# Seven products instead of eight for the first token block of a gated layer, with weight differences and the last normalizations moved to VectorE

## The chip, the core and the metric

The kernel runs on one core of a Trainium2 chip, in fp32 throughout. The metric is the device time of one execution in microseconds (us), the median of several runs. Five engines work beside each other, each with its own queue in program order: TensorE (PE; its weight loads are shown apart as PEld), VectorE (DVE), ScalarE (ACT), GpSimd (POOL) and SyncE (SP), which issues most of the DMAs.

## The reference

The computation is one transformer block on x of 2 x 1024 tokens by 256, with a context of 2 x 154 by 192 and 16 heads of 64: self attention, cross attention, and a gated feed-forward layer with 1024 hidden columns.

```python
h = _layernorm(x, ln1_g, ln1_b)
x = _attention(h, h, sa_wq, sa_wk, sa_wv, sa_wo, sa_bo) + x
h = _layernorm(x, ln2_g, ln2_b)
x = _attention(h, cond_emb, ca_wq, ca_wk, ca_wv, ca_wo, ca_bo) + x
h = _layernorm(x, ln3_g, ln3_b)
p = h @ ff_w1 + ff_b1
a, gate = (p[..., :D_FF], p[..., D_FF:])
h = a * jax.nn.gelu(gate, approximate=False) @ ff_w2 + ff_b2
return h + x
```

The change touches the last three lines of the layer: the third normalization for the second batch element, and the product with `ff_w2` for the first quarter of the tokens.

## The kernel before, in words

The order of all instructions is written out by hand (`manual_schedule`): what the Python code calls first stands first in each engine's queue. Self attention runs first, then cross attention, then the gated layer, which is a loop over 64 steps `k`. Pieces of neighbouring stages are put into the steps: the first steps still finish the cross attention and its output projection (`out_piece`, added to x by VectorE at L473), and the third normalization of the second batch element runs at steps 7 to 19.

The tokens are taken in four blocks ("pairs") of 512, each of two halves of 256 (`BT`). The hidden columns are taken in eight chunks of 128, so chunk `n` of the run from 0 to 31 is hidden chunk `n % 8` of block `n // 8`. Chunk `n` takes step 2n (`gate_first`) and step 2n + 1 (`gate_second`), and its last product comes in step 2n + 2 (`gate_last`).

The first projection forms, for both halves and for the value and gate columns, a 2 x 2 scheme of block products with seven products in place of eight (L1062), which needs sums and differences of the weights (`weight_sums`) and of the tokens (`token_sums`, four GpSimd instructions, L1045 to L1048). Their results are joined outside TensorE. ScalarE copies the first product (L1081) and does the two Gelus (L1099, L1105). VectorE does the additions: L1085 and L1087 in `gate_first`, L1101 and L1104 in `gate_second`, L1113 in `gate_last`. The products accumulate in the same PSUM banks, so TensorE's second product into a bank comes after VectorE has read the first. GpSimd multiplies value by gate for the second half (L1106) and for the first half (L1115), into the tiles `ub`.

The second projection multiplies the hidden columns by `ff_w2`. For blocks 1 to 3 it is done in seven products as well (`partial`): the 2 x 2 scheme is over even and odd hidden chunks and over the two halves of the output columns. It needs four differences of quarters of `w2` (`column_sums`, 128x512 each, GpSimd, L1153, at steps 18, 20, 24 and 26) and, for every block and every two hidden chunks, four sums of hidden tiles (`row_sums`, GpSimd, L1165 to L1168). For each of two token tiles a product is four matmuls with 128 columns (L1186), and after the products 1, 6, 3 and 7 VectorE adds parts of the result to x (L1195). Block 0 is done in the plain way: for each of four token tiles eight matmuls of 256 columns (L1225), one addition (L1235) and one store. `sums` is the list of this work, and each step takes slots from its front: two matmuls a step for block 0 (steps 16 to 31), one product a step for the later blocks (from step 32).

The buffer for the differences and row sums (`hold_sums`, tile `wx`) takes the place of a ring buffer of the cross attention, which is read for the last time in step 5.

The third normalization of the second batch element has four parts, a pair of token tiles at a time: statistics on VectorE (`stats`, L239 and L240), variance and deviation on GpSimd (`deviation`, L245 and L249), an offset on VectorE (L255) with scale and shift on GpSimd (`normalize`, L266), and the transposes on TensorE (`turn`, L279), whose results ScalarE scales (L294). A pair passes these parts in steps two apart: statistics of the first pair at step 7, deviation at 9, normalization at 11, transposes at 13. The bias of the layer is added to x by GpSimd (L319), one token tile every third step from 13 on.

Of the kernel before, what the change touches and what calls it, by code (L numbers as in the profile page):

```python
# [8 lines left out]
F32 = mybir.dt.float32  # L9
AF = mybir.ActivationFunctionType  # L10
ALU = mybir.AluOpType
AX = mybir.AxisListType

P = 128
# [4 lines left out]
def tile_transformer_block(ctx: ExitStack, tc: tile.TileContext, a: dict, out: bass.AP):  # L19
    nc = tc.nc  # L20
# [3 lines left out]
    B, S, D = x.shape  # L24
# [7 lines left out]
    NT = S // P  # L32
    GT = 4
# [17 lines left out]
    NF = DF // P  # L51
    SH = GH // 2
    TF = 2
# [18 lines left out]
    def sum_tile(name):  # L72

        return ps_o.tile([P, HB], F32, tag="po", name=name)
# [22 lines left out]
    for n in names:  # L97
        k = n_of[n]
# [121 lines left out]
    def norm_pieces(kind, b, first=False):  # L220
# [7 lines left out]
        st = {}  # L228
# [22 lines left out]

        def normalize(t):
            rstd = st["rstd", t]
            off = small.tile([P, 2], F32, tag="off", name=f"off_{ln}_{b}_{t}")
            nc.vector.scalar_tensor_tensor(  # L255
                off, st["mv", t][:, :, 0], -1.0, rstd, op0=ALU.mult, op1=ALU.mult
            )
            pool, tag = (one, "xn") if narrow(kind, b) and not first else (pp_, "P")

            xn = pool.tile([P, nh, 2, D // nh], F32, tag=tag, name=f"xn_{ln}_{b}_{t}")  # L260
            st["xn", t] = xn
            for i in range(2):
                xs = xt[b, order[t + i] // GT][:, order[t + i] % GT, :]
                xs, own = xs.rearrange("p (c d) -> p c d", c=nh), xn[:, :, i, :]
                if not narrow(kind, b) or first and i == 1:
                    nc.gpsimd.tensor_scalar(  # L266
                        own, xs, rstd[:, i:i + 1], off[:, i:i + 1], op0=ALU.mult, op1=ALU.add)
                else:
                    nc.scalar.activation(
                        own, xs, AF.Identity, bias=off[:, i:i + 1], scale=rstd[:, i:i + 1])  # L270
# [837 lines left out]
    def gate_last(n):  # L1108

        pair, f = divmod(n, NF)  # L1110
        pa, pb, pc, own = psum.pop(n)
        product(n, 4, pb, False)
        nc.vector.scalar_tensor_tensor(  # L1113
            own[:, 0, :], pb[:, :BT], biases(n)[0], own[:, 0, :], op0=ALU.add, op1=ALU.add)
        nc.gpsimd.tensor_tensor(ub[pair][0][:, f, :], own[:, 0, :], own[:, 3, :], ALU.mult)  # L1115
        if f == NF - 1:
            if pair:
                early, late = (1, 4, 2), (5, 6, 3, 7)
                if pair == NPR - 1:
                    sums.extend((pair, i, m) for m in early for i in range(TF))  # L1120
                    sums.extend((pair, i, m) for i in range(TF) for m in late)
                else:
                    sums.extend((pair, i, m) for i in range(TF) for m in early + late)
            else:
                sums.extend((pair, i, e) for i in range(2 * TF) for e in range(NF))

    sums, summed = [], {}

# [21 lines left out]
    def column_sums(n):  # L1150

        t = half["t"]
        nc.gpsimd.tensor_tensor(*[  # L1153
            lambda: (t[5], quarter(0, 1), quarter(0, 0)),
            lambda: (t[6], quarter(1, 1), t[5]),
            lambda: (t[4], quarter(1, 0), t[6]),
            lambda: (t[7], quarter(1, 1), quarter(0, 1)),
        ][n](), ALU.subtract)

    def row_sums(pair, c):  # L1160

        s = {i: own[:, c, :] for i, own in half["s"][pair % 2].items()}
        (a11, a12), (a21, a22) = ([ub[pair][j][:, 2 * c + e, :] for e in range(2)] for j in range(2))
        tt = nc.gpsimd.tensor_tensor
        tt(s[5], a21, a22, ALU.add)  # L1165
        tt(s[6], s[5], a11, ALU.subtract)
        tt(s[3], a12, s[6], ALU.subtract)
        tt(a21, a11, a21, ALU.subtract)  # L1168
# [46 lines left out]

    def sum_slot():

        pair, i, f = sums.pop(0)
        if pair:
            return partial(pair, i, f)  # L1220
        if f == 0:
            summed[pair] = sum_tile(f"pf{pair}_{i}")
        own = summed[pair]
        j, e = divmod(i, TF)
        nc.tensor.matmul(  # L1225
            own[:, :D], lhsT=ub[pair][j][:, f, e * P:(e + 1) * P], rhs=w2[:, f, :],
            start=(f == 0), stop=(f == NF - 1),
        )
        if f < NF - 1:
            return None  # L1230
        b, t = divmod(pair * 2 * TF + i, NT)

        def store():
            xs = xt[b, t // GT][:, t % GT, :]
            nc.vector.tensor_tensor(xs, own[:, :D], xs, ALU.add)  # L1235
            nc.sync.dma_start(out=out[b, t * P:(t + 1) * P, :], in_=xs)

        return store


    with tc.manual_schedule():
# [192 lines left out]
        for k in range(2 * FU):  # L1434
# [16 lines left out]
                out_pieces("ca", B - 1, NQ - 1, out_order("ca"))  # L1451
            if k % (2 * NF) == NF and k < 2 * FU - 2 * NF:
                token_sums(k // (2 * NF) + 1)
            for _ in range(min(2 if k < 4 * NF else 1, len(sums))):
                run(sum_slot)
            flush(stores)
            run_work(0 if k in (1, 2 * len(CG) - 1) else 1 + k % 2, k % 2)
            if later and k > 12 and k % 3 == 1:
                later.pop(0)()
            if k == 2 * NF:  # L1460
                hold_sums()
            if k in (2 * NF + 2, 2 * NF + 4, 2 * NF + 8, 2 * NF + 10):
                column_sums((k - 2 * NF) // 3)
            pair, at = divmod(k - 5, 2 * NF)
            if pair > 0 and at % 4 == 0:
                row_sums(pair, at // 4)
# [38 lines left out]
```

## Time and profile before

| | us |
|---|---|
| median of the runs (3) | 1084.04 |
| lowest and highest run | 1083.71, 1085.92 |
| the profiled execution | 1085.11 |
| its span in the profile | 1083.3 |
| TensorE busy in the span | 1067.4 (99%) |
| VectorE, ScalarE, GpSimd busy | 889.9, 646.9, 765.0 |

The profile is one execution. Times in its timelines and windows are microseconds from the start of the span. A line such as L1062 is a line of the kernel before; a name such as `own<-pb` tells which tile is written from which. In a timeline a row gives the start, the duration, the engine, the line, the operation, the tiles, the shapes and the count, and in brackets the idle time before it with what ended it. A 256-wide fp32 product of the program appears as two matmul records.

### The profile page before, as it was taken

The numbers are of one execution on the slowest core, as the hardware profiler recorded it, in microseconds if no ns is written. First come the engines' busy times: TensorE is split into PE (matmuls) and PEld (weight loads), VectorE is DVE, ScalarE is ACT, GpSimd is POOL, SyncE is SP. The second block draws the span as 40 slices with busy tenths as digits, with TensorE's granted clock in tenths as the row PEclk, the third lists the DMA queues.
The fourth block names the chain that finished last, engine by engine and source line by source line (L and its number), as shares of the span: only waits on it lengthen the run. The fifth ranks groups of instructions, "written<-read, shape, count | busy, mean of one in ns | idle before, by whom it ended". The sixth has DMA issues, their size and how long they took to land.

```text
span 1083.3 us, 45246 instructions
## 1 busy us (share of the span) xinstructions
PE 1067.4 (99%) x18548; PEld 710.0 (66%) x18548; DVE 889.9 (82%) x1317; ACT 646.9 (60%) x2063; POOL 765.0 (71%) x1600
## 2 busy tenths in 40 slices
PE   8999999999999999999999999998999999999998
PEld 6556556566565565565675665575777767888998
DVE  5789999998998989999999989968877887655554
ACT  5666767677666666666776766666566554342221
POOL 2667777788777777777777777757665686388774
PEclk9999999999999999999999999999999999999999
DMA  3232111111111111211211201136855545000000
GB/s 94 64 90 62 44 43 44 37 38 43 33 43 24 43 43 33 48 42 29 48 41 26 53 14 37 24 96 139 202 134 138 126 115 131 17 6 15 20 11 30
DMA packets 105120, 62.84 MB, mean 58 GB/s; under 512 B 32266, under 2 KB 95506, under 8 KB 104914
## 3 DMA queue, kind: packets, MB, share of 16 engines
q1 hardware_dynamic: 103586, 59.29, 23.2%
q8 instruction: 146, 2.39, 0.9%
q10 hardware_dynamic: 1328, 0.66, 0.2%
q14 instruction: 60, 0.49, 0.1%
HBM read 30.01 MB, written 2.10 MB: 30 GB/s over the span
## 4 chain that ended last, share of the span: by engine, by line
PE 87%; DVE 3%; DMA 3%; POOL 3%; ACT 2%; SPq 1%; issue 1%; DVEq 0%; POOLq 0%; ACTq 0%
PE s L492 19%; PE po L546 19%; PE py_sa L466 5%; PE py_ca L466 5%; PE pv_sa L392 5%; PE pq_ca L361 4%; PE pq_sa L361 4%; PE pk_sa L361 4%; PE poc L938 4%; PE pb L1062 3%; PE pf L1186 3%; PE sc L855 3%; PE pa L1062 2%; PE pc L1062 2%; DMA st<-st 2%; PE pf L1225 1%
## 5 line engine op out<-in xcount | busy, mean ns | idle before, releaser
L612 POOL TENSOR_SCALAR p<-p,rd,ee 128x512 f32<-128x512 f32 x508 | 387.3, 773 | 99.1 <-DVE rd L604 97.3
L507 ACT ACTIVATE p<-s,st 128x512 f32<-128x512 f32 x512 | 345.8, 686 | 176.5 <-DVE st L501 170.5
L501 DVE TENSOR_REDUCE st<-s 128x2 f32<-128x1024 f32 x256 | 308.5, 1206 | 51.7 <-issue 20.1
L639 DVE STREAM_TRANSPOSE pT<-p 128x1024 f32<-128x1024 f32 x256 | 302.3, 1219 | 1.5 <-POOL p L612 1.5
L492 PE MATMUL s<-k_sa,q_sa 64*32 64x512 f32 x4096 | 255.4, 591 | 2.7 <-ACT p L507 2.1
L546 PE MATMUL po<-pT,v_sa 64*32 64x256 f32 x8192 | 238.6, 376 | 0.9 <-ACT p L873 0.9
L546 PEld LDWEIGHTS po<-pT,v_sa 64*32 64x32 f32 x8192 | 173.8, 106 | 74.9 <-issue 27.3
L492 PEld LDWEIGHTS s<-k_sa,q_sa 64*32 64x32 f32 x4096 | 81.6, 106 | 102.8 <-issue 53.5
L873 ACT ACTIVATE p<-sc,neg 128x154 f32<-128x154 f32 x256 | 96.5, 408 | 84.5 <-DVE rden L881 80.7
L884 POOL TENSOR_SCALAR p<-p,rden 128x154 f32<-128x154 f32 x256 | 97.3, 401 | 62.7 <-DVE rden L881 62.3
L507 ACT ACTIVATION_READ_ACCUMULATOR p<-s,st 128x1 f32 x512 | 103.2, 202 | 0.0
L525 POOL TENSOR_TENSOR dd<-st 128x8 f32<-128x8 f32 x128 | 25.8, 202 | 66.1 <-DMA st<-st 64.3
L392 PEld LDWEIGHTS pv_sa<-sa_wv,hT_ln 64*128 64x128 f32 x1024 | 58.6, 188 | 14.2 <-issue 10.9
L392 PE MATMUL pv_sa<-sa_wv,hT_ln 64*128 64x128 f32 x1024 | 61.8, 275 | 0.0
L860 DVE TENSOR_REDUCE neg<-sc 128x6 f32<-128x924 f32 (+1 forms) x48 | 48.0, 1001 | 14.5 <-PE sc L855 14.4
L466 PE MATMUL py_ca<-ca_wo,o_ca 128*128 128x256 f32 x256 | 59.9, 382 | 0.0
L466 PE MATMUL py_sa<-sa_wo,o_sa 128*128 128x256 f32 x256 | 59.5, 386 | 0.0
L466 PEld LDWEIGHTS py_sa<-sa_wo,o_sa 128*128 128x128 f32 x256 | 47.3, 190 | 17.8 <-issue 6.9
L361 PE MATMUL pq_ca<-hT_ln,ca_wq 64*128 64x512 f32 (+1 forms) x352 | 58.4, 590 | 0.5 <-DMA ca_wq<-in_L_xattn_ca_wq_dram 0.5
L873 ACT ACTIVATION_READ_ACCUMULATOR p<-sc,neg 128x1 f32 x256 | 57.2, 224 | 0.0
L361 PE MATMUL pq_sa<-hT_ln,sa_wq 64*32 64x512 f32 (+1 forms) x976 | 57.0, 586 | 0.0
L361 PE MATMUL pk_sa<-hT_ln,sa_wk 64*32 64x512 f32 x960 | 56.8, 590 | 0.0
(135 smaller groups left out, 1471.5 us busy)
## 6 DMA issues: line engine op xcount, KB each, us to landing
wf<-pT_ca SPq DMA_DIRECT2D x128, 128.0 KB, 2.4
v_sa<-v_sa SPq DMA_DIRECT2D x32, 256.0 KB, 3.8
st<-st SPq DMA_DIRECT2D x510, 1.0 KB, 1.9
sa_wq<-in_L_xattn_sa_wq_dram SPq DMA_DIRECT2D x32, 128.0 KB, 3.4
sa_wk<-in_L_xattn_sa_wk_dram SPq DMA_DIRECT2D x32, 128.0 KB, 3.6
sa_wv<-in_L_xattn_sa_wv_dram SPq DMA_DIRECT2D x32, 128.0 KB, 3.3
ca_wq<-in_L_xattn_ca_wq_dram SPq DMA_DIRECT2D x32, 128.0 KB, 4.4
wf<-in_L_xattn_ff_w_dram SPq DMA_DIRECT2D x12, 256.0 KB, 4.2
```

The costliest lines, as they stand in the source:

```text
L361: nc.tensor.matmul(pq[r][f:f + m, at:at + n], lhsT=wt[own, c, f:f + m], rhs=h[own, c, t0:t0 + n], start=(c == 0), stop=(c == NH - 1), tile ...
L392: nc.tensor.matmul(pv[r][:, i * P:(i + 1) * P], lhsT=h[own, c, i * P:(i + 1) * P], rhs=wt[own, c, :], start=(c == 0), stop=(c == NH - 1), ...
L466: nc.tensor.matmul(py[:, e * D:(e + 1) * D], lhsT=o[:, i, (t + e) * P:(t + e + 1) * P], rhs=wo[kind, b, g][:, i, :], start=(i == 0), stop= ...
L492: nc.tensor.matmul(sc[a4 * KB:(a4 + 1) * KB, j, :], lhsT=q[r, c:c + KB], rhs=k[r, h * HB:(h + 1) * HB], start=True, stop=True, tile_positi ...
L501: nc.vector.tensor_reduce(st[:, 0, 0, i, :], sc, AX.X, ALU.max, negate=True)
L507: nc.scalar.activation(pr[:, j, :], sc[:, j, :], AF.Exp, bias=st[:, 0, 0, i, j:j + 1], accum_out=st[:, 0, 1, i, j:j + 1],)
L546: nc.tensor.matmul(po[a2][d:d + KB, :QH // 2], lhsT=v[r, t, e, d:d + KB], rhs=pT[r, d // DH * NK + n, :], start=(t == 0 and e == 0), stop= ...
L612: nc.gpsimd.tensor_scalar(pr[:, j, :], pr[:, j, :], v["rd"][:, c:c + 1], v["ee"][:, 0, c:c + 1], op0=ALU.mult, op1=ALU.mult,)
L639: nc.vector.transpose(halves[h][:, :, c:c + KB], slot[p]["members"][i].rearrange("p j (n k) -> p (j n) k", k=KB))
L873: nc.scalar.activation(pr_[:, j, i, :T], sc[:, j, i * T:(i + 1) * T], AF.Exp, bias=neg[:, j, i:i + 1], accum_out=den[:, j, i:i + 1],)
L884: nc.gpsimd.tensor_scalar(pr_[:, j, i, :T], pr_[:, j, i, :T], rden[:, j, i:i + 1], 1.0, op0=ALU.mult, op1=ALU.mult,)
L1062: nc.tensor.matmul(into[:, :BT], lhsT=lhs, rhs=wh[pair][i], start=first, stop=True, skip_group_check=True)
```

## The change

The first block's second projection is done in seven products like the others. Its 32 matmuls of 256 columns become 56 of 128 columns, in 14 slots of one product each (steps 16 to 29), the four additions on VectorE become twelve, and the plain path is removed. The row sums of block 0 are added on GpSimd, at steps 8, 10, 14 and 17, four instructions each.

The buffer `wx` is taken at step 7 instead of 16. The four differences of `w2` are done by VectorE instead of GpSimd, at the ends of steps 7, 9, 11 and 13 instead of 18, 20, 24 and 26.

The normalization of the second batch element ahead of the gated layer subtracts the mean and multiplies by the deviation on VectorE, two instructions for a pair of token tiles, in place of one offset on VectorE and two instructions on GpSimd. It stands where the offset stood, at steps 11, 13, 15 and 17.

```diff
         def normalize(t):
             rstd = st["rstd", t]
+            if kind == "ff" and b == B - 1:
+                xn = st["xn", t] = pp_.tile(
+                    [P, nh, 2, D // nh], F32, tag="P", name=f"xn_{ln}_{b}_{t}")
+                for i in range(2):
+                    xs = xt[b, order[t + i] // GT][:, order[t + i] % GT, :]
+                    nc.vector.tensor_scalar(
+                        xn[:, :, i, :], xs.rearrange("p (c d) -> p c d", c=nh),
+                        st["mv", t][:, i, 0:1], rstd[:, i:i + 1],
+                        op0=ALU.subtract, op1=ALU.mult)
+                return
...
         if f == NF - 1:
-            if pair:
-                early, late = (1, 4, 2), (5, 6, 3, 7)
-                if pair == NPR - 1:
-                    sums.extend((pair, i, m) for m in early for i in range(TF))
-                    sums.extend((pair, i, m) for i in range(TF) for m in late)
-                else:
-                    sums.extend((pair, i, m) for i in range(TF) for m in early + late)
+            early, late = (1, 4, 2), (5, 6, 3, 7)
+            if pair == NPR - 1:
+                sums.extend((pair, i, m) for m in early for i in range(TF))
+                sums.extend((pair, i, m) for i in range(TF) for m in late)
             else:
-                sums.extend((pair, i, e) for i in range(2 * TF) for e in range(NF))
+                sums.extend((pair, i, m) for i in range(TF) for m in early + late)
...
     def column_sums(n):
 
         t = half["t"]
-        nc.gpsimd.tensor_tensor(*[
+        nc.vector.tensor_tensor(*[
...
     def sum_slot():
 
-        pair, i, f = sums.pop(0)
-        if pair:
-            return partial(pair, i, f)
...
+        return partial(*sums.pop(0))
...
-            for _ in range(min(2 if k < 4 * NF else 1, len(sums))):
+            for _ in range(min(1, len(sums))):
                 run(sum_slot)
...
-            if k == 2 * NF:
+            if k == NF - 1:
                 hold_sums()
-            if k in (2 * NF + 2, 2 * NF + 4, 2 * NF + 8, 2 * NF + 10):
-                column_sums((k - 2 * NF) // 3)
+            if k in (NF - 1, NF + 1, NF + 3, NF + 5):
+                column_sums((k + 1 - NF) // 2)
+            if k in (NF - 1 + 1, NF + 2, NF + 6, 2 * NF + 1):
+                row_sums(0, (k + 1 - NF) // 3)
```

More of the change, by code (lines that the diff above doesn't have):

```diff
@@ L1216, in sum_slot @@
     def sum_slot():
-        pair, i, f = sums.pop(0)
-        if pair:
-            return partial(pair, i, f)
[L1221 to L1238, printed above, removed]
+        return partial(*sums.pop(0))
     with tc.manual_schedule():
```

## The prediction

> **What bounds the kernel now.** I read the page first, then a table of windows over the gated layer, then the chain of waits through it, and last the timelines of TensorE (PE), VectorE (DVE) and GpSimd (POOL) between 930 and 1000 us.
>
> ```profile
> span 1083.3 us, 45246 instructions
> ...
> PE 1067.4 (99%) x18548; PEld 710.0 (66%) x18548; DVE 889.9 (82%) x1317; ACT 646.9 (60%) x2063; POOL 765.0 (71%) x1600
> ```
>
> TensorE is busy 99% of the span, so a time saved anywhere else shows only where TensorE waits. The windows (stretch, length, then busy time of PE, PEld, DVE, ACT, POOL) say where that is:
>
> ```profile
> 942.10:953.80 11.70, 10.92 (x51) 8.23 (x50) 10.13 (x32) 4.80 (x12) 9.34 (x17) 1.00 0.01 1
> 955.50:994.50 39.00, 39.00 (x186) 34.33 (x186) 19.52 (x46) 13.01 (x29) 34.64 (x49) 1.00 0.04 13
> 994.50:1027.00 32.50, 32.50 (x207) 30.10 (x206) 18.65 (x44) 9.13 (x20) 23.35 (x34) 1.00 0.04 15
> ```
>
> From 955.5 on TensorE has no idle time: the first block's sixteen slots of the second projection and the next block's fourteen are bound by its matmuls. Between 942.1 and 953.8, hidden chunks 4 to 7, whose steps have no second projection to fill them, it is idle 0.78 of 11.70 us, while VectorE is busy 10.13 and GpSimd 9.34. The timeline of VectorE shows why:
>
> ```profile
> 941.88 0.48 DVE L1101 SCALAR_TENSOR_TENSOR own<-pb,cols,own 128x256 f32<-128x256 f32 x1 [0.17 <-PE pb L1062]
> ...
> 945.30 0.48 DVE L1101 SCALAR_TENSOR_TENSOR own<-pb,cols,own 128x256 f32<-128x256 f32 x1 [0.46 <-PE pb L1062]
> ...
> 947.15 0.37 DVE L255 SCALAR_TENSOR_TENSOR off_ln<-mv_ln,rstd_ln 128x2 f32<-128x2 f32 x1
> 947.44 0.47 DVE L1113 SCALAR_TENSOR_TENSOR own<-pb,cols,own 128x256 f32<-128x256 f32 x1
> 947.84 0.41 DVE L1085 TENSOR_TENSOR own<-pb,own 128x256 f32<-128x256 f32 x1
> ...
> 949.04 0.48 DVE L1101 SCALAR_TENSOR_TENSOR own<-pb,cols,own 128x256 f32<-128x256 f32 x1 [0.46 <-PE pb L1062]
> ...
> 950.89 0.37 DVE L255 SCALAR_TENSOR_TENSOR off_ln<-mv_ln,rstd_ln 128x2 f32<-128x2 f32 x1
> ...
> 952.88 0.48 DVE L1101 SCALAR_TENSOR_TENSOR own<-pb,cols,own 128x256 f32<-128x256 f32 x1 [0.44 <-PE pb L1062]
> ...
> 953.65 0.43 DVE L255 SCALAR_TENSOR_TENSOR off_ln<-mv_ln,rstd_ln 128x2 f32<-128x2 f32 x1
> 954.87 0.48 DVE L1113 SCALAR_TENSOR_TENSOR own<-pb,cols,own 128x256 f32<-128x256 f32 x1 [0.80 <-PE pb L1062]
> ...
> 958.23 0.73 DVE L255 SCALAR_TENSOR_TENSOR off_ln<-mv_ln,rstd_ln 128x2 f32<-128x2 f32 x1
> 960.06 0.48 DVE L1113 SCALAR_TENSOR_TENSOR own<-pb,cols,own 128x256 f32<-128x256 f32 x1 [1.09 <-PE pb L1062]
> ```
>
> L1101 of chunk 5 starts at 945.30 and of chunk 6 at 949.04, and all that VectorE does between stands back to back: L1101, L1104, the norm's statistics, the offset L255, L1113, L1085, L1087. TensorE waits for the L1085 in it:
>
> ```profile
> 948.30 0.70 PE L1062 MATMUL pb<-hT_ln,wf 128*128 128x256 f32 x2 [0.45 <-DVE own L1085]
> ...
> 949.70 0.55 PE L279 MATMUL ph_ln<-ident,xn_ln 128*128 128x128 f32 x3 [0.16 <-POOL xn_ln L266]
> ...
> 957.69 1.03 PE L1225 MATMUL pf<-wf,u 128*128 128x256 f32 x4
> ...
> 960.72 1.03 PE L1225 MATMUL pf<-wf,u 128*128 128x256 f32 x4
> ```
>
> L1085 ends at 948.26, the product into the same bank starts at 948.30, and its end lets L1101 start at 949.04. That is a loop: VectorE's work from L1101 to L1085, plus 0.78 us of TensorE's answer. It takes 945.30 - 941.88 = 3.42 us for chunk 4, 3.74 for chunk 5 and 3.84 for chunk 6, where seven products of 0.43 us are 3.0. Each VectorE instruction put into it lengthens the kernel by its whole time. From chunk 7 on there is slack: L1113 at 954.87 waited 0.80 us and at 960.06 1.09 us for TensorE.
>
> **The change, part by part.** First the second projection of the first block. The chain has the price of a slot in both forms (start, length, group):
>
> ```profile
> 948.55 1.11 POOL xn_ln L266 x2
> ...
> 955.70 0.86 PE pf L1225 x4
> ...
> 991.97 0.86 PE pf L1225 x4
> ...
> 994.56 0.89 PE pf L1186 x8
> ```
>
> A slot of the plain form is two 256-wide matmuls, 0.86 us, and there are 16 of them, 13.76 us. A slot of the seven-product form is four 128-wide ones, 0.89 us, and there are 14, 12.46 us. On a TensorE without idle time that is -1.30 us. The narrower stores on VectorE (twelve additions in place of four) lie in steps that have the same slots in the next block, where the window from 994.5 shows TensorE busy throughout, so I cost them at nothing; without that cover each would be in VectorE's slack of some 1.3 us a step.
>
> Second, the four weight differences (128x512 each) go from GpSimd to VectorE, to the ends of steps 7, 9, 11 and 13, behind the gate of chunks 3, 4, 5 and 6. The one at step 7 stands before two residual additions that wait for TensorE's output projection anyway: nothing. The other three stand in the loop. No row has this operation on VectorE; the nearest are these groups (count, busy us and mean ns):
>
> ```profile
> L1195 DVE TENSOR_TENSOR x<-pf,x 128x512 f32<-128x512 f32 x12 | 8.3, 692 | 6.2 <-PE pf L1186 6.2
> ...
> L290 DVE TENSOR_SCALAR hT_ln<-ph_ln,cols 128x256 f32<-128x256 f32 x6 | 3.0, 531 | 0.0
> ...
> L810 DVE MEMSET v_ca<- 128x512 f32 x2 | 1.0, 485 | 0.1
> ```
>
> The same operation with one operand in PSUM takes 0.69 us, a mere 128x512 fill 0.485. I take 0.60, with 0.485 and 0.69 as ends. Beside it there is a wait. The offset L255 reads two tensors in SBUF, as the differences do. In the cross attention, under short GpSimd instructions, it took 0.18 us:
>
> ```profile
> 878.99 0.18 DVE L255 SCALAR_TENSOR_TENSOR off_ln<-mv_ln,rstd_ln 128x2 f32<-128x2 f32 x1
> ```
>
> In the gated layer it took 0.37, 0.37 (at 950.89, as at 947.15), 0.43 and 0.73 us, and GpSimd's rows tell when it came free:
>
> ```profile
> 938.99 0.73 POOL L1115 TENSOR_TENSOR u<-own 128x256 f32<-128x256 f32 x1 [3.11 <-DVE own L1113]
> ...
> 946.78 0.73 POOL L1106 TENSOR_TENSOR kT<-own 128x256 f32<-128x256 f32 x1 [0.94 <-ACT own L1105]
> 947.58 0.19 POOL L245 TENSOR_SCALAR var_ln<-mv_ln 128x2 f32<-128x2 f32 x1
> 947.85 0.69 POOL L249 TENSOR_TENSOR rstd_ln<-var_ln,power 128x2 f32<-128x2 f32 x1
> ...
> 953.33 0.73 POOL L319 TENSOR_TENSOR x<-x,ff_b 128x256 f32<-128x256 f32 x1
> ...
> 958.23 0.73 POOL L319 TENSOR_TENSOR x<-x,ff_b 128x256 f32<-128x256 f32 x1
> ...
> 970.00 0.72 POOL L1165 TENSOR_TENSOR wx<-u 128x256 f32<-128x256 f32 x1
> ...
> 972.98 0.73 POOL L1115 TENSOR_TENSOR u<-own 128x256 f32<-128x256 f32 x1
> ```
>
> The one at 947.15 ends at 947.52, GpSimd's L1106 at 946.78 + 0.73 = 947.51. The one at 953.65 ends at 954.08, L319 at 954.06. The one at 958.23 ends at 958.96 together with L319. So VectorE is held until the running GpSimd instruction ends. The mean of the four is 0.475, so the wait is 0.30 us, and I give that to each difference: 0.90 us. (The Trainium skill, page "SBUF — State Buffer", section "Who interferes with whom", says the same: a VectorE instruction with two SBUF inputs and a GpSimd one that reads SBUF exclude each other for the whole instruction. The rows agree to 0.02 us.)
>
> Third, the last four normalizations. Each pair of GpSimd's L266 (1.10 us) becomes two VectorE instructions of 128x256 with two per-partition scalars, in place of one offset. Nearest is L290, the same kind and size from PSUM: 0.53 us alone; with some overlap I take 0.45 each, no wait, ends 0.18 (the offset) and 0.53. What goes is L255, 0.29 us of spacing (947.15 to 947.44), and TensorE's wait of 0.16 us for L266 at 949.70; the latter is worth nothing, since VectorE's loop and not that wait set the next L1101. The page "VectorE: DVE Perf Modes" of the Trainium skill, section "Mode 2×_2P", lets a fp32 instruction of this kind with SBUF operands do two elements a cycle, but through the port that GpSimd shares. By it a half would be some 0.3 us plus the 0.30 us wait, 1.2 a pair instead of 0.90, and the sum below 0.6 us higher.
>
> Loop by loop: chunk 4, one difference, +0.90. Chunk 5, a pair and a difference less the offset, 0.90 + 0.90 - 0.29 = +1.51. Chunk 6, the same, +1.51. Chunk 7, a pair less its offset, 0.90 - 0.43 = 0.47, within the slack of 0.80: nothing. Chunk 8, 0.90 - 0.73 = 0.17, within 1.09: nothing. Together +3.92.
>
> Fourth, GpSimd's queue. Sixteen row sums of the first block come in (steps 8, 10, 14, 17), the differences and normalizations leave. Laid end to end from L1115 of chunk 3 at 938.99 up to L1115 of chunk 7: four token sums 2.9 us (0.73 each), twelve row sums 8.9 (972.98 - 970.00 = 2.98 for four), nine gate products and a bias at 0.69 spacing 6.9, four variance and deviation pairs at 0.96 (947.58 to 948.55) 3.8; end 961.6, and 963.4 if three differences hold it up 0.60 each. The queue now carries the deviation L249, for which VectorE's normalization waits, behind the row sums: the second deviation ends at 952.6 laid so, about 953.2 with one hold by a difference, and VectorE asks for it at 950.89 + 0.90 + 1.51 = 953.3: just in time. TensorE's slot at step 17 (957.69 before) asks for chunk 7's L1106 with its last matmul, at 957.69 + 3.92 + 0.67 = 962.3; that L1106 ends 0.73 + 0.96 us before the 963.4, at 961.7. The slot at step 18 (960.72) asks for L1115 at 965.3. So GpSimd costs nothing, with 0.6 us of slack, and what it is late with next would be step 17. DMA: the four output stores of the block stay four, on SP, at steps 21, 22, 28, 29 in place of 19, 23, 27, 31, and nothing on SP waits behind them that TensorE needs; the buffer of the differences is wanted at step 7, two steps after its last reader.
>
> Sum: -1.30 + 3.92 = +2.6 us. The profiled execution took 1085.11 us (span 1083.3), 1.07 above the median of the runs, so the sum gives 1087.7 for it and 1086.6 beside the median of 1084.04.
>
> **Ends.** Low: differences at 0.485 without wait, normalization halves 0.18: 0.49 + 2 x (0.36 + 0.49 - 0.29) = 1.6, less 1.30, +0.3. Below that only if the additions fall in idle time, which the back-to-back rows of the loop exclude. High: 0.69 + 0.30 for a difference, (0.53 + 0.30) x 2 for a pair, so chunk 4 +0.99, chunks 5 and 6 +2.36 each, chunk 7 1.66 - 0.43 - 0.80 = +0.43: 6.1, less 1.30, +4.8.
>
> **Rivals.** (A) The additions are cheap: no hold by GpSimd, VectorE faster from SBUF than from PSUM. Then it is the low end, +0.3, 1084.3. For it: no row shows these two instructions. Against: the offsets' ends. (B) The port for the normalizations too, or GpSimd bound: held instructions push its queue past the 0.6 us of slack and TensorE waits at step 17. From there each us of delay is a us of time; with the high end +4.8, 1088.8. For it: GpSimd is laid end to end for 22 us; against: the loop's lengthening gives it time. (C) Faster: if GpSimd's L266 and not VectorE sets the pace of chunks 4 to 6, its removal frees 3.42 + 3.74 + 3.84 less three times 3.02 and one set of transposes (0.43), 1.5 us, and the additions hide: -2.8, 1081.2. It decides if L1101 there waits for TensorE after a transpose, not after L1085; the row at 948.30 names L1085.
>
> **How the numbers follow.** Measurement tells 0.2%, 2.2 us, from no change. The forecast (between +1.4 and +3.9, +2.6 likeliest) gets 0.48, A 0.28, B 0.18, C 0.06. Slower by more than 0.2%: B and 0.34 of the forecast, 0.52; within: A and the forecast's rest, 0.42; faster: C, 0.06. The range from 1084.0 to 1088.9 leaves out C, A's lower edge and B's upper half.
>
> **What would show it.** Right: TensorE at 0.89 a slot from step 16 on; the loop of chunk 4 near 4.3 us and of chunks 5 and 6 near 5.3; differences that end when a GpSimd instruction has ended. Wrong: loops as long as before (A or C), TensorE idle before the slots of steps 16 to 19 with GpSimd as releaser (B), or VectorE waiting for L249 ahead of a normalization.

## The result and the profile after

The changed kernel takes 1089.31 us, the median of 5 runs from 1088.18 to 1090.36, beside 1084.04 before: by the means of the runs 1.0042 times as long, 95% interval 1.0028 to 1.0057. Its profiled execution took 1089.31 us with a span of 1087.5. Measured a second time it took 1087.24 beside 1084.28 (1.0031, 1.0020 to 1.0042). So it is slower; the prediction was +2.6 us, and the medians of the two measurements gave +5.3 and +3.0. The first median lies 0.4 us above the upper end of the stated range, 1088.9; the second lies inside.

Part of the difference between the two kernels arises ahead of the instructions that the change touches. Up to the gate of chunk 3 the two kernels issue nearly the same work, yet that point lies at 933.68 us in the trace before, at 935.01 in the first trace after and at 933.20 in the second; over all kernels here it lies anywhere between 930.6 and 935.0. In the first trace after, the timeline of GpSimd shows where the 1.3 us came in, a small transfer that landed late; in the second trace after, the same instruction has no wait:

```profile
697.45 0.20 POOL L535 TENSOR_TENSOR dd<-st 128x8 f32<-128x8 f32 x1 [2.04 <-DMA st<-st]
```
```profile
695.25 0.20 POOL L535 TENSOR_TENSOR dd<-st 128x8 f32<-128x8 f32 x1
```

From the gate of chunk 3 to that of chunk 31 both traces of the changed kernel take 134.99 us, the kernel before 132.12. **The change costs 2.87 us**, and that is the figure to explain. (The first comparison adds up: 2.87, and 1.33 from before chunk 3, make the 4.20 us between the two profiled executions, 1085.11 and 1089.31; the other 1.07 is what the profiled execution before lay above its median.) Page of the profile after:

```profile
span 1087.5 us, 45364 instructions
...
PE 1069.3 (98%) x18596; PEld 708.8 (65%) x18596; DVE 898.5 (83%) x1331; ACT 645.9 (59%) x2063; POOL 765.1 (70%) x1604
```

VectorE has 8.6 us more to do (898.5, was 889.9), GpSimd as much as before (765.1, was 765.0). TensorE's busy share hardly moved, from 98.5 to 98.3% of the span. Its timeline shows the new waits, all at the same place as the 0.45 us before, at the product that must follow VectorE's L1095 (L1085 before):

```profile
946.74 0.70 PE L1072 MATMUL pb<-hT_ln,wf 128*128 128x256 f32 x2 [0.97 <-DVE own L1095]
...
951.93 0.70 PE L1072 MATMUL pb<-hT_ln,wf 128*128 128x256 f32 x2 [1.91 <-DVE own L1095]
952.47 0.91 PE L1072 MATMUL pc<-hT_ln,w1s 128*128 128x256 f32 x2
953.17 1.06 PE L289 MATMUL ph_ln<-ident,xn_ln 128*128 128x128 f32 x4
954.02 1.06 PE L1072 MATMUL pa<-hT_ln,wf 128*128 128x256 f32 x2
954.88 1.06 PE L1072 MATMUL pb<-hs,wf 128*128 128x256 f32 x2
...
957.91 0.70 PE L1072 MATMUL pb<-hT_ln,wf 128*128 128x256 f32 x2 [0.57 <-DVE own L1095]
```

VectorE's timeline shows what stands in the loop (L1111 is the gate, L1101 before; L1160 the weight difference; L259 the normalization, two halves in one row, so that the duration is that of the pair):

```profile
943.22 0.48 DVE L1111 SCALAR_TENSOR_TENSOR own<-pb,cols,own 128x256 f32<-128x256 f32 x1 [0.17 <-PE pb L1072]
...
945.07 0.89 DVE L1160 TENSOR_TENSOR wx<-wf,wx 128x512 f32<-128x512 f32 x1
...
947.48 0.48 DVE L1111 SCALAR_TENSOR_TENSOR own<-pb,cols,own 128x256 f32<-128x256 f32 x1 [0.46 <-PE pb L1072]
...
949.33 1.23 DVE L259 TENSOR_SCALAR xn_ln<-x,mv_ln,rstd_ln 128x256 f32<-128x256 f32 x2
950.47 0.68 DVE L1160 TENSOR_TENSOR wx<-wf,wx 128x512 f32<-128x512 f32 x1
...
952.67 0.48 DVE L1111 SCALAR_TENSOR_TENSOR own<-pb,cols,own 128x256 f32<-128x256 f32 x1 [0.46 <-PE pb L1072]
953.41 0.42 DVE L1114 TENSOR_TENSOR own<-pc,own 128x256 f32<-128x256 f32 x1 [0.26 <-PE pc L1072]
...
954.74 0.18 DVE L240 BATCH_NORM_AGGREGATE mv_ln<-st_ln 128x2 f32<-128x6 f32 x1
954.99 1.54 DVE L259 TENSOR_SCALAR xn_ln<-x,mv_ln,rstd_ln 128x256 f32<-128x256 f32 x2
956.45 0.68 DVE L1160 TENSOR_TENSOR wx<-wf 128x512 f32<-128x512 f32 x1
...
958.65 0.48 DVE L1111 SCALAR_TENSOR_TENSOR own<-pb,cols,own 128x256 f32<-128x256 f32 x1 [0.46 <-PE pb L1072]
...
959.42 1.55 DVE L259 TENSOR_SCALAR xn_ln<-x,mv_ln,rstd_ln 128x256 f32<-128x256 f32 x2
```

The rows of L1111 are the gates of chunks 4 (943.22), 5, 6 and 7 (958.65), so the loops of chunks 4, 5 and 6 take 4.26, 5.19 and 5.98 us. Before they took 3.42, 3.74 and 3.84. The first normalization did not wait for its deviation L249. The one at 954.99 did, briefly: VectorE was free at 954.92, the deviation ended at 954.95, and the normalization began 0.04 us later. Back to back, as at 949.33, it would have begun some 0.16 us earlier. GpSimd's timeline:

```profile
944.68 0.73 POOL L1173 TENSOR_TENSOR wx<-wx,u 128x256 f32<-128x256 f32 x1
945.49 1.06 POOL L1174 TENSOR_TENSOR wx<-u,wx 128x256 f32<-128x256 f32 x1
...
949.63 0.77 POOL L1172 TENSOR_TENSOR wx<-kT 128x256 f32<-128x256 f32 x1
950.48 1.26 POOL L1173 TENSOR_TENSOR wx<-wx,u 128x256 f32<-128x256 f32 x1
...
954.25 0.70 POOL L249 TENSOR_TENSOR rstd_ln<-var_ln,power 128x2 f32<-128x2 f32 x1
954.92 0.72 POOL L1125 TENSOR_TENSOR u<-own 128x256 f32<-128x256 f32 x1
955.61 0.78 POOL L1116 TENSOR_TENSOR kT<-own 128x256 f32<-128x256 f32 x1
956.45 0.73 POOL L245 TENSOR_SCALAR var_ln<-mv_ln 128x2 f32<-128x2 f32 x1
```

A row sum normally takes 0.73 us. Three of GpSimd's rows are longer: L1174 with 1.06 and L1173 with 1.26 beside a difference on VectorE, and L245 with 0.73 (normally 0.19) beside another. So the two engines hold each other up, in both directions. The normalizations are held by whatever runs on GpSimd: the pair at 949.33 ends about 0.15 us after the row sum L1172 (949.63 + 0.77), the pair at 954.99 as long after the gate product L1116 (955.61 + 0.78). In both traces each of the eight halves ends 0.15 us after the end of a GpSimd instruction that ran beside it, be it a gate product, a row sum or a bias addition.

### The profile page after: what moved, and what is told of

It reads as the page before. It is cut to its first block, busy times and chain, and to the rows that moved or that the text cites. A ratio compares the mean times of both kernels' runs of the same rounds, so it can differ in the third digit from the quotient of the medians.

```text
span 1087.5 us, 45364 instructions
## 1 busy us (share of the span) xinstructions
PE 1069.3 (98%) x18596; PEld 708.8 (65%) x18596; DVE 898.5 (83%) x1331; ACT 645.9 (59%) x2063; POOL 765.1 (70%) x1604
## 4 chain that ended last, share of the span: by engine, by line
PE 85%; POOL 4%; DVE 3%; DMA 3%; ACT 2%; issue 1%; SPq 1%; DVEq 0%; POOLq 0%; ACTq 0%
PE s L502 18%; PE po L556 18%; PE py_sa L476 5%; PE pv_sa L402 5%; PE py_ca L476 5%; PE pk_sa L371 5%; PE pf L1193 4%; PE pq_sa L371 4%; PE pq_ca L371 4%; PE poc L948 4%; PE pb L1072 3%; PE sc L865 3%; PE pa L1072 2%; PE pc L1072 2%; DMA st<-st 2%
## 5 line engine op out<-in xcount | busy, mean ns | idle before, releaser
L502 PEld LDWEIGHTS s<-k_sa,q_sa 64*32 64x32 f32 x4096 | 79.4, 106 | 104.6 <-issue 58.4
```

The lines of the kernel that those rows point to most:

```text
L502: nc.tensor.matmul(sc[a4 * KB:(a4 + 1) * KB, j, :], lhsT=q[r, c:c + KB], rhs=k[r, h * HB:(h + 1) * HB], start=True, stop=True, tile_positi ...
```

## The experiments

Two theories were put against each other. V: the time is in VectorE's loop, in the instructions that VectorE got and in their being held while GpSimd works. G: it is in GpSimd's queue, where the row sums now stand ahead of the deviation and the gate products that others wait for. Each kernel was timed beside the kernel before on the same chip. The table gives, in us and for the profiled execution, the loops of chunks 4, 5 and 6 (from one start of L1111 or L1101 to the next) and the stretch from chunk 3's to chunk 31's.

| kernel | time, before beside it | ratio (95%) | loops 4, 5, 6 | chunk 3 to 31 |
|---|---|---|---|---|
| before | | | 3.42, 3.74, 3.84 | 132.12 |
| after | 1089.31, 1084.04 | 1.0042 (1.0028 to 1.0057) | 4.26, 5.19, 5.98 | 134.99 |
| after, again | 1087.24, 1084.28 | 1.0031 (1.0020 to 1.0042) | 4.26, 5.50, 5.67 | 134.99 |
| normalizations on GpSimd | 1089.92, 1084.70 | 1.0054 (1.0041 to 1.0066) | 4.26, 4.32, 10.41 | 138.54 |
| differences early on GpSimd | 1086.08, 1084.70 | 1.0012 (1.0003 to 1.0021) | 3.42, 5.10, 5.46 | 133.54 |
| row sums late | 1086.44, 1084.70 | 1.0020 (1.0011 to 1.0029) | 4.26, 4.81, 4.81 | 133.80 |
| row sums behind the deviation | 1086.92, 1084.21 | 1.0025 (1.0015 to 1.0035) | 4.26, 6.22, 5.61 | 135.64 |
| before, normalizations on VectorE | 1085.72, 1084.28 | 1.0008 (1.0000 to 1.0017) | 3.42, 4.19, 4.19 | 132.68 |
| before, normalization late | 1084.76, 1084.28 | 1.0003 (0.9994 to 1.0012) | 3.02, 3.02, 3.03 | 132.48 |
| seven products alone | 1091.43, 1085.01 | 1.0058 (1.0044 to 1.0072) | 3.42, 3.74, 3.84 | 140.08 |
| late, early and ScalarE | 1084.62, 1084.70 | 0.9999 (0.9990 to 1.0008) | 3.03, 3.02, 3.02 | 131.91 |
| late and early | 1081.55, 1084.28 | 0.9976 (0.9966 to 0.9985) | 3.02, 3.03, 3.02 | 129.63 |

### The changed kernel again

No edit.

> The changed kernel once more, to settle how much of its measured 5.3 us lies outside the gated layer. In its profile the stretch from chunk 3 to the end is 2.9 us longer than before, and 1.3 us had been lost by then, in code that is the same in both, at one 1 KB exchange of the self attention that landed 2 us late near 695 us. If that is chance of single executions, the time is 2.9 us over the kernel before, 0.27%. If the shifted program makes it systematic, it stays near 5 us and the profile shows the stretch ahead of chunk 3 longer again.

1087.24 us. The stretch from chunk 3 on takes what it took in the first trace, to 0.01 us (only the split between chunks 5 and 6 differs); the rest of the difference is ahead of it. The first comparison's +5.3 us held about 2 us that did not come again.

### The normalizations back on GpSimd

```diff
-            if kind == "ff" and b == B - 1:
+            if False:
                 xn = st["xn", t] = pp_.tile(
```

> The changed kernel with its last normalizations back on GpSimd (offset on VectorE, scale and shift on GpSimd). Theory V, VectorE's queue sets the pace of chunks 4 to 6: the loop of chunk 5 loses 1.14 us of normalization and gains 0.37 of offset, that of chunk 6 1.46 and 0.37, so 4.4 and 4.9 us in place of 5.19 and 5.98, about 1.9 us faster than the changed kernel, 1087.4. Theory G, GpSimd's queue with the row sums in front of the deviations sets it: GpSimd gets 1.1 us more for each pair, the first pair's normalization stands behind eight row sums and ends near 954, TensorE's transposes ask for it near 951 and wait some 3 us; no gain or a loss against the changed kernel, 1089 to 1091.

The kernel became slower than the changed one, by 3.55 us in the gated layer, as theory G had it (1089 to 1091, V 1087.4). VectorE's loop of chunk 5 shrank to 4.32, but in that of chunk 6 TensorE stands before the transposes, since the first normalization (L276) comes behind the row sums in GpSimd's queue. TensorE's waits between 936 and 985 us (engine, line, releaser, us in total, times, longest):

```profile
PE ph_ln L289 <- POOL xn_ln L276: 3.8, 1, 3.8
```

So GpSimd's queue is full in these steps: with the row sums where the change puts them, the normalizations have to leave it. That part of the change saves more than it costs.

### The differences early on GpSimd

```diff
-        nc.vector.tensor_tensor(*[
+        nc.gpsimd.tensor_tensor(*[
...
-            if k == NF - 1:
+            if k == NF - 3:
                 hold_sums()
-            if k in (NF - 1, NF + 1, NF + 3, NF + 5):
-                column_sums((k + 1 - NF) // 2)
+            if k in (NF - 3, NF - 2):
+                for i in range(2):
+                    column_sums(2 * (k + 3 - NF) + i)
```

> The changed kernel with its four weight differences back on GpSimd, but at the ends of steps 5 and 6, two each, where GpSimd had idle time of 3 us a chunk. Theory V: the loops of chunks 4, 5 and 6 lose 0.81, 0.61 and 0.61 us, 2.0 us in all, 1087.3. Theory G: GpSimd loses only the holds of 0.33 and 0.53 us, and chunk 6 waits for the second deviation as before: 0.9 us, 1088.4. Either: if GpSimd is not done with the differences by step 8, its queue starts the row sums up to 1 us later.

The gated layer gains 1.45 us over the changed kernel (133.54 against 134.99), between V's 2.0 and G's 0.9. The loop of chunk 4 is back at 3.42. Those of chunks 5 and 6 become shorter by only 0.61 together, because the pair of halves takes 1.53 and 1.54 us there, and the second one waits 0.48 us for its deviation: without the difference VectorE comes sooner, waits longer for the deviation behind the row sums, and then runs beside GpSimd all the same.

### The row sums late

```diff
-            for _ in range(min(1, len(sums))):
+            for _ in range(min(1 if k >= 2 * NF + 2 else 0, len(sums))):
...
-            if k in (NF - 1 + 1, NF + 2, NF + 6, 2 * NF + 1):
-                row_sums(0, (k + 1 - NF) // 3)
+            if 2 * NF - 2 <= k < 2 * NF + 2:
+                row_sums(0, k + 2 - 2 * NF)
```

> The changed kernel with the row sums of the first block at steps 14 to 17 in place of 8, 10, 14, 17, and the first block's slots from step 18 on (two steps later; the list had two empty steps before the next block). Chunks 4 to 6 then have VectorE's additions without GpSimd's row sums beside them. Theory V with VectorE's own times: differences 0.68, a pair of halves near its unheld 1.0, loops 4.1, 5.1 and 5.2 against 4.26, 5.19, 5.98, a gain of 1.0 us there. Theory G: the deviations come early, the loops fall to 4.1, 4.4, 4.4, a gain of 2.5 us there. In both, steps 18 to 22 may give back up to 3 us, since GpSimd has twelve row sums to do just before them.

With no row sums in their steps the loops of chunks 5 and 6 take 4.81 each, 1.55 less together (V had 1.0, G 2.5 for the three loops), and the first two pairs 0.82 us each. The third and fourth, which now meet the row sums, take 1.48 and 1.61. VectorE's timeline:

```profile
947.61 0.82 DVE L259 TENSOR_SCALAR xn_ln<-x,mv_ln,rstd_ln 128x256 f32<-128x256 f32 x2
...
952.42 0.82 DVE L259 TENSOR_SCALAR xn_ln<-x,mv_ln,rstd_ln 128x256 f32<-128x256 f32 x2
...
956.15 1.48 DVE L259 TENSOR_SCALAR xn_ln<-x,mv_ln,rstd_ln 128x256 f32<-128x256 f32 x2
...
960.00 1.61 DVE L259 TENSOR_SCALAR xn_ln<-x,mv_ln,rstd_ln 128x256 f32<-128x256 f32 x2
```

### The row sums behind the deviation

If only the order in GpSimd's queue mattered, it should help to put the row sums behind the deviation of each step, at steps 9, 11, 15 and 17.

```diff
-            if k in (NF - 1 + 1, NF + 2, NF + 6, 2 * NF + 1):
-                row_sums(0, (k + 1 - NF) // 3)
+            if k in (NF + 1, NF + 3, 2 * NF - 1, 2 * NF + 1):
+                row_sums(0, (k - NF) // 3 if k < 2 * NF else 3)
```

> The changed kernel with the row sums of the first block at steps 9, 11, 15, 17 in place of 8, 10, 14, 17, so that each set stands behind the deviation that is made in the same step and not in front of it. GpSimd still does eight row sums beside the loops of chunks 4 to 6. Theory V with holds (VectorE's instructions wait for the row sum that runs): the loops stay, chunks 5 and 6 together at 10.5 to 11.3 us against 11.17 in the changed kernel and 9.62 with the row sums moved to step 14 and later. Theory G (the deviation comes late behind the row sums): they fall to 9.6 to 10.0. The differences, 0.68 us, and the first loop, 4.2 us, stay in both.

The loops of chunks 5 and 6 take 11.83 together, more than the 11.17 of the changed kernel and above both expectations. The deviations are there in time, but now the pair and the difference behind it both run beside GpSimd's row sums and gate products. The pair takes 1.34 and the difference 1.20 us. (Some 0.75 us of the 11.83 are extra waits of L1111 and L1114 for a TensorE at half clock after a wait of 2.55 us, 0.26 in the changed kernel; see the last section.) The third pair, which meets an idle GpSimd (957.95 to 958.73), takes 0.73:

```profile
947.27 1.34 DVE L259 TENSOR_SCALAR xn_ln<-x,mv_ln,rstd_ln 128x256 f32<-128x256 f32 x2
948.53 1.20 DVE L1160 TENSOR_TENSOR wx<-wf,wx 128x512 f32<-128x512 f32 x1
...
958.02 0.73 DVE L259 TENSOR_SCALAR xn_ln<-x,mv_ln,rstd_ln 128x256 f32<-128x256 f32 x2
```

So the order in the queue is not what lengthens these loops, apart from the 0.16 us in the changed kernel; being beside GpSimd's work is. The same pair of instructions takes 0.73 beside nothing and 1.2 to 1.6 beside a full queue. By these rows the row sums lengthen it by filling the gaps of that queue, also where a gate product is what runs beside the pair.

### The kernel before with the normalizations on VectorE

The third part of the change alone: the new branch of `normalize` (as in the diff of the change), put into the kernel before.

> The kernel before with the normalizations alone on VectorE, no row sums of the first block and no differences beside them. Theory V with holds by GpSimd's running instruction: a pair costs 1.1 to 1.5 us in place of the offset's 0.29, the loops of chunks 5 and 6 are 4.5 to 5.0, together 1.7 to 2.3 us more, chunk 7 within its slack; 1.5 to 2 us slower than before. Theory G: without row sums GpSimd has gaps, the halves run near 0.3 to 0.5 each, the loops are 4.1 to 4.4, 0.7 to 1.2 us more; and the 0.16 us wait of TensorE is gone in both.

The loops of chunks 5 and 6 grow by 0.45 and 0.35, the pairs take 0.82 and later 0.73. That is G's range (0.7 to 1.2 together) and not V's (1.7 to 2.3), which took a full hold for granted: without the row sums GpSimd has gaps. Groups of VectorE's instructions between 940 and 975 us, of this kernel and of the changed one (count, busy us, mean ns of a half, idle time before):

```profile
L259 DVE TENSOR_SCALAR xn_ln<-x,mv_ln,rstd_ln 128x256 f32<-128x256 f32 x8 | 3.1, 429 | 0.0
```
```profile
L259 DVE TENSOR_SCALAR xn_ln<-x,mv_ln,rstd_ln 128x256 f32<-128x256 f32 x8 | 5.9, 772 | 0.3 <-POOL rstd_ln L249 0.2
```

A half takes 0.43 us on the mean here and 0.77 in the changed kernel: the same instruction on the same data.

### The kernel before with the normalization late

The gated layer's steps 16 and later have a slot of the second projection, so VectorE has slack there. Here the four parts of the normalization begin at step 15 instead of 7.

```diff
-            if k == 2 * len(CG) + 1:
+            if k == 2 * NF - 1:
                 norm_beside
```

> The kernel before with one edit: the third normalization of the second batch element begins at step 15 in place of 7. It takes VectorE's statistics and offsets out of the loops of chunks 4 to 6. Theory V (VectorE's queue sets these loops): 3.02 us each in place of 3.42, 3.74 and 3.84, a gain of 2.0 us there; GpSimd, which is busy 34.6 of 39 us from step 16 on, gets deviations and normalizations on top there and gives some back by late transposes at steps 23 to 27, 1 to 2 us. If TensorE's wait for GpSimd's normalization set the loops and not the statistics: chunk 4, which has none of these waits, keeps its 3.42.

The loops of chunks 4 to 6 fall to 3.02, seven products of 0.43, which is TensorE's own time. But over chunks 4 to 13, which hold the four sets of transposes in both kernels, the loops take 45.31 us together, 44.95 before. The gain is given back in chunks 12 and 13 (5.94 and 6.55, where chunk 11 takes 5.19), whose normalizations come late in GpSimd's queue: the one for chunk 12 behind row sums of the second block, the one for chunk 13 behind token sums and a difference (L1153, 1.27 us). TensorE's waits between 936 and 1010 us:

```profile
PE ph_ln L279 <- POOL xn_ln L266: 1.1, 3, 0.7
```

### The seven products alone

The normalizations back on GpSimd, the differences early on GpSimd and the row sums late, by the three edits above together; VectorE gets nothing new but the narrower additions.

> The seven-product form for the first block alone: the differences are on GpSimd (two each at the ends of steps 5 and 6), the normalizations on GpSimd with the offset on VectorE as in the kernel before, the row sums of the first block at steps 14 to 17 and its slots from step 18. Theory V (the additions to VectorE and its contention with GpSimd cost the time, the seven-product form itself saves its 1.30 us): the loops of chunks 4, 5 and 6 are 3.4, 3.7 and 3.8 as in the kernel before (11.0 together), and the time is 0.3 to 1.5 us under the kernel before. Rival G (GpSimd cannot hold row sums and normalizations together at steps 14 to 17): normalizations and gate products come late behind the row sums, TensorE waits 1 us or more for GpSimd between steps 15 and 19, and the time is equal to the kernel before or up to 2 us above it.

Slower than everything else. The loops of chunks 4 to 6 are those of the kernel before, so what those loops lost in the changed kernel comes from VectorE's additions and the row sums beside them, and from nothing else in the change. But the loops of chunks 8 and 9 take 9.29 and 9.57 instead of 5.19 and 5.19, by the mechanism of G, though G allowed a loss of 2 us at most: the third and fourth normalization come behind row sums. Of the 8.48 us, 5.4 are waits of TensorE; in the rest its clock stood at 0.50 for 3.4 us beside each of the two long waits (see the last section). The waits, and the transposes with what follows them:

```profile
PE ph_ln L289 <- POOL xn_ln L276: 5.4, 4, 3.1
```
```profile
959.35 1.44 PE L289 MATMUL ph_ln<-ident,xn_ln 128*128 128x128 f32 x4 [3.08 <-POOL xn_ln L276]
960.59 1.06 PE L1072 MATMUL pa<-hT_ln,wf 128*128 128x256 f32 x2
...
968.45 0.33 PE L289 MATMUL ph_ln<-ident,xn_ln 128*128 128x128 f32 x1 [1.99 <-POOL xn_ln L276]
...
969.50 1.06 PE L1072 MATMUL pa<-hT_ln,wf 128*128 128x256 f32 x2
```

So the saving of the seven products is lost with the row sums at steps 14 to 17 and the rest of GpSimd's queue as it was; something has to leave it or move in time.

### Late, early and ScalarE

The differences early on GpSimd, the normalization begun at step 15, and its scale and shift on ScalarE instead of VectorE (the new branch of `normalize` is off, as in the run with the normalizations on GpSimd):

```diff
-                if not narrow(kind, b) or first and i == 1:
+                if not narrow(kind, b) and not (kind == "ff" and b == B - 1) or first and i == 1:
```

> Seven products for the first block with nothing added to VectorE: differences on GpSimd at the ends of steps 5 and 6, the third normalization of the second batch element begun at step 15 in place of 7 (its statistics and deviations then lie beside the slots of the second projection), scale and shift on ScalarE. Theory V and theory G both expect the loops of chunks 4 to 6 at TensorE's 3.02 us each, 1.9 us under the kernel before, and 1.3 us from the fourteen slots: 1081 to 1082. If the gain of the slots were an artefact of the profile, only the 1.9 us would show, 1082.2; if the later normalization is late for the token sums of step 24, TensorE waits at step 32 and the gain is lost.

The loops of chunks 4 to 6 are at 3.02, but the time that both theories gave, 1081 to 1082, did not come: the gain of 1.93 us there is given back in the next ones (6.25 for chunk 8 and 6.67 for chunk 10, where the kernel before has 5.19 and 4.75). TensorE waits 1.17 us in a slot for GpSimd's gate product, which comes behind row sums, and 1.12 us for L1091, which now stands behind normalizations in ScalarE's queue:

```profile
PE pf L1193 <- POOL kT L1116: 1.2, 1, 1.2
PE pa L1072 <- ACT own L1091: 1.1, 1, 1.1
```

### Late and early

The changed kernel with the differences early on GpSimd, the normalization begun at step 15 (on VectorE as in the change), and the first slot at step 17:

```diff
-            for _ in range(min(1, len(sums))):
+            for _ in range(min(1 if k > 2 * NF else 0, len(sums))):
```

> The changed kernel with three edits: differences on GpSimd at the ends of steps 5 and 6, the third normalization (on VectorE) begun at step 15, the first block's slots from step 17 in place of 16. Nothing is left in the loops of chunks 4 to 6 but the gate: 3.02 us each, 1.9 us under the kernel before, and 1.3 us from the slots. The run with ScalarE lost 1.2 us to chunk 7's L1116 behind the row sums of step 14 and 2.5 us to ScalarE's normalizations waiting for deviations; the later start of the slots takes the first, VectorE's slack of 1.3 us a step most of the second. Both theories: 2 to 2.6 us under the kernel before, 1082.3.

1081.55 us, 0.9976 times the kernel before (0.9966 to 0.9985): it beats both kernels, the changed one by 5.36 us in its gated layer (129.63 against 134.99). The pairs of halves still take 1.15 to 1.60 us beside GpSimd, but where they stand VectorE has the slack of a slot, and one wait of 0.2 us is all that TensorE has left between 936 and 1010 us:

```profile
PE pb L1072 <- DVE own L1095: 0.2, 1, 0.2
```

## Why the prediction came out as it did

The sum was +3.92 - 1.30 = +2.6 us, and the gated layer lost 2.87. The mechanism, VectorE's loop between L1111 and L1095 in the steps without slots, is the one that the trace shows. That the two numbers lie so close is in part luck: the loops lost 0.51 us more than forecast, and the rest gave back 0.26 more. Inside the loops the pairs were priced 0.97 us too low and two differences some 0.4 too high. The terms:

- **The slots.** 0.89 us each, as forecast. Outside the loops of chunks 4 to 6 the stretch from chunk 3 on became 1.56 us shorter (119.56 against 121.12): the 1.30 predicted, and 0.26 of idle time in the loop of chunk 7 before (4.58 against 3.02 for seven products, 0.44 for transposes and 0.86 for the slot), which is gone after (4.35). The additions on VectorE are ten for the block, five for each pair of token tiles, and not the twelve of the prediction; they cost TensorE nothing, as forecast.
- **The loops.** Forecast +0.90, +1.51 and +1.51; measured +0.84, +1.45 and +2.14 (+0.84, +1.76 and +1.83 in the second trace), together +4.43 instead of +3.92. Chunks 7 and 8 cost nothing, as forecast.
- **The differences.** 0.60 us and 0.30 of being held were forecast. They take 0.69 unheld, which is the upper end that the prediction gave, 0.89 in chunk 4, where one is held, and 0.68 in chunks 5 and 6, where GpSimd's instruction beside it is the one that is held (the 1.26 and the 0.73 in the rows above). The sum of 0.90 was right for one of the three loops. Even the held one did not end with GpSimd's row sum, as the prediction gave for a sign, but 0.55 us after it.
- **The normalizations.** This is the step that failed: "some overlap I take 0.45 each, no wait". 0.45 was right for a half beside little work (0.43 in the kernel before with them on VectorE). Beside a GpSimd queue without gaps a pair took 1.23, 1.54, 1.55 and 1.55 us, where 0.90 was forecast, because each half was held until a GpSimd instruction had ended. The alternative that the prediction stated, 0.3 us a half and 0.30 of wait, is borne out as to the wait; its 1.2 us a pair fits the first pair of this trace and not the others. Its speed rests on the section "Mode 2×_2P" of the Trainium skill's page "VectorE: DVE Perf Modes", by which such an instruction does two elements a cycle when its tensors lie in SBUF. As to that speed, a half takes about 0.4 us with GpSimd idle, 0.37 by the pair of 0.73 at 958.02, not 0.3.
- **GpSimd.** "So GpSimd costs nothing" was right as far as TensorE's slots go: none waited for it, and the queue was not late at step 17. VectorE did wait for L249, which the prediction had named as a sign of being wrong: 0.16 us at step 13 and 0.23 at step 17, the latter outside the three loops. The sentence was wrong in leaving out what GpSimd's work does to VectorE: without row sums in steps 8 to 13 the loops of chunks 5 and 6 are 1.55 us shorter. The table's values for these two loops together show how the parts stand to each other: 7.58 before, 8.38 with the normalizations, 9.62 with the differences too, 10.56 with row sums instead of the differences, 11.17 with all. The differences cost 1.24 us without the row sums and 0.61 beside them, the row sums 2.18 or 1.55; the shares can't be added one by one.
- **TensorE's wait of 0.16 us for L266**, now gone, did not set the loops, as forecast: they grew without it. Rival C is excluded: L1111 still waits for the product behind L1095. Rival B was right that the normalizations are held and wrong about the place, since TensorE did not wait at step 17.

The median of the first comparison lies 2.7 us above the forecast and 0.4 above the range. The gated layer accounts for 0.3 of that, the rest arose ahead of it and in how the profiled execution before stood to its median. A range built from terms of the change alone leaves such shifts out; the medians of two sets of runs of this same kernel lie 2.07 us apart.

## What to carry to other kernels

The price of some instructions on VectorE depends on what GpSimd does beside them. A fp32 normalization of 128x256 from SBUF to SBUF took about 0.4 us with GpSimd idle and up to 0.9 beside its full queue. The statistics (L239, one tensor read from SBUF) and the gate's additions (one operand in PSUM) kept their 0.39 to 0.42 and 0.41 to 0.48 us beside the same queue. So an instruction moved from the one to the other is to be priced beside what stays or is added there. Look first for the steps where the engine that gets the work has slack: the normalizations that lengthen VectorE's loops in steps 11 and 13 cost TensorE a wait of 0.2 us in all once they start at step 19, among the slots, held by GpSimd as they are (in the kernel that has the differences early as well). And a saving on TensorE that puts 16 instructions more on a full queue has to be counted together with the place where those instructions go.

## What the runs showed of the hardware that was not expected

**Each wait of TensorE of 1.9 us or more came with half the clock.** After the wait of 1.91 us the products in the timeline above come 0.86 us apart (954.02 and 954.88) instead of 0.43, and the windows of the changed kernel (us from the start, length, busy time of PE, PEld, DVE, ACT and POOL, granted clock, DMA share, GB/s) show the clock at half for some 3.4 us:

```profile
951.00:952.00 1.00, 0.07 (x1) 0.07 (x1) 1.00 (x4) 0.00 (x0) 0.92 (x2) 1.00 0.00 0
952.00:953.00 1.00, 1.00 (x4) 0.80 (x5) 0.54 (x2) 0.00 (x0) 1.00 (x2) 0.81 0.00 0
953.00:954.00 1.00, 1.00 (x5) 0.83 (x4) 0.74 (x3) 0.13 (x1) 0.93 (x3) 0.50 0.07 16
...
955.00:956.00 1.00, 1.00 (x4) 0.82 (x3) 1.00 (x2) 0.83 (x3) 1.00 (x2) 0.50 0.00 0
956.00:957.00 1.00, 1.00 (x6) 0.83 (x5) 1.00 (x2) 0.47 (x2) 0.93 (x2) 0.98 0.00 0
```

In the gated layer of all kernels here, six waits of 1.90 us or more (1.90, 1.91, 1.99, 2.55, 3.08, 3.82) were followed by a granted clock of 0.50, which in the two longest began before the wait had ended, and none of those of 1.80 or less (1.80, 1.74, 1.52, 1.17 and shorter). What sets the point between the two the runs do not show. What it cost in the changed kernel is small, because TensorE had to wait for VectorE again afterwards: L1114 of chunk 6 waited 0.26 us for it (953.41 in VectorE's timeline above). In the second trace L1111, which usually waits 0.46 us, and L1114 waited 0.68 us more than usual:

```profile
951.16 0.48 DVE L1111 SCALAR_TENSOR_TENSOR own<-pb,cols,own 128x256 f32<-128x256 f32 x1 [0.77 <-PE pb L1072]
952.01 0.42 DVE L1114 TENSOR_TENSOR own<-pc,own 128x256 f32<-128x256 f32 x1 [0.37 <-PE pc L1072]
```

No term of the prediction had it. (The Trainium skill, page "TensorE: Matmul & The Clock Gate", section "Why this matters for your kernels", warns of gaps over about 3 us; here the trace shows the drop to half at 1.9 us.)

**The hold goes both ways, and the engine that waits is not always VectorE.** Beside differences GpSimd's row sums took 1.06 and 1.26 us instead of 0.73, and a 128x2 addition 0.73 instead of 0.19; beside GpSimd's gate products and row sums VectorE's pair went from 0.73 to 1.55. Which of the two is held went, in these two rows, by which started first: the difference at 945.07 ended 0.55 us after the row sum at 944.68 had, and the difference at 950.47, which began 0.01 us before GpSimd's L1173, took its usual 0.68. At 956.45, where both rows start within 0.01 us, GpSimd's was the one held.
